# Deformable convolution plus attention on one core: five sample buffers and a second transposed chunk at the start of the first batch

## The chip, the cores and the metric

The kernel runs on one core of one Trainium2 chip, written in a tile language that schedules five engines: TensorE (PE), VectorE (DVE), ScalarE (ACT), GpSimd (POOL) and SyncE (SP, which here only issues DMAs). The metric is the device time of one execution in microseconds (us). Before the change three runs took 7757.02, 7759.71 and 7764.04 us; their median is 7759.71.

## The reference

The input is x of shape (4, 128, 64, 64) in fp32. For each batch (cut to what matters):

```
offset, mask = conv3x3(x, w_off), sigmoid(conv3x3(x, w_mask))   # after GroupNorm of x
samples      = bilinear_sample(x, grid + offset) * mask          # 9 taps, 4 corners each
x2           = x + einsum('bckhw,ock->bohw', samples, w) + bias  # deformable conv, residual
t            = layernorm(tokens of x2)                           # 4096 tokens of 128
q = k = v    = cosine / cumulative-product features of t         # 16 heads of 8
a            = softmax(q k^T / sqrt(8)) v                        # over all 4096 tokens
y            = combine, layernorm, FFN, then top-2 of 8 experts  # out has the shape of x
```

## The kernel before

**Preparing a batch.** `prepare(b)` (L784) loads x, runs `group_norm`, writes a table of corner pairs to DRAM (`corner_table`, L450 to L481), computes for each of 4096 positions and 9 taps a table row and four weights (`offsets`, in two halves of 16 blocks; L483 to L561), and then samples (`deform`, L563). The table takes 16 DMAs of 256 KB, from four row blocks `tok`; those of batch 0 go partly through ScalarE's queue, behind the loads of the weights (`load`, `load_bc`, L283 to L291, and L303 to L340), and the fourth `tok` must wait for one of three `v` buffers (L468). Ahead of `deform`, batch 0 also runs `settle` (L384): some VectorE operations on weights that the FFN needs.

**Units.** `deform` walks over 96 units: 8 chunks of 512 positions, in each 3 groups of 3 taps and 4 blocks of 128 positions. A unit, called u0, u1 and so on here, is three indirect DMAs that POOL issues (L575, 256 KB each, two units ahead, into one of three `v` buffers), a VectorE multiply by the weights (L589), and two adds (L591, L592). Then, in chunk 0 of batch 0, TensorE transposes the three taps (L600) and VectorE copies them into `sT_first` (L601). In all other chunks VectorE makes three 32x32 stream transposes (L617), SP writes the result to DRAM (`smd`, L630; four puts per group) and reads it back transposed (`sT`, L663; four loads per group).

**Chunks.** When a chunk's 12 units are done, `convolved` (L647) runs the nine-tap conv on TensorE (L273), adds the residual (`xr`, L689), normalizes (`x2`, `xt`; POOL raises to the power -0.5, L376), and `features` (L723) makes the rows `rn` on VectorE, the value rows `fx` on POOL (L754), then TensorE transposes `rn` (`fT_ps`, L767) and VectorE splits the result in `hiT` and `loT` (L769, L770). SP writes these to `kTd` and `qTd` (L777, L778), from where attention loads keys `kT` (L1156), queries `qT` (L1166) and values `qf` (L1158). All of TensorE's small work shares one PSUM bank (`misc`).

**Attention.** A step is one block of 128 keys against 512 queries for four heads: four matmuls into `sc` (L1178), two exponentials on ScalarE (L1187), four matmuls into `acc` (L1195). There are 3700 steps in all, 964 in the first batch. Batch 0's steps begin while its later chunks are still being prepared: step 0 needs chunk 0, step 16 chunk 1, step 64 chunk 2, step 104 chunk 3; this opening ends with step 160, and steps 256, 260, 288 and 292 need chunks 4 to 7.

**What sets the order.** A planner, `Beside`, steps through the attention and fits the other work between. Each piece declares its cost with `need(pe=, dve=, lat=, after=)`; `later` puts an emission off to a planned time, and `hold` keeps pieces of one PSUM bank together. The order that comes out is written for PE, DVE, SP and POOL, in the program's order (`tc.manual_schedule`); ScalarE's order is a scheduler's. Each engine runs its own list in order. DMAs share eight semaphore slots, and a DMA waits for the one eight before it.

Of the kernel before, what the change touches and what calls it, by code (L numbers as in the profile page):

```python
# [9 lines left out]
F32 = mybir.dt.float32  # L10
# [193 lines left out]
def ve(n, ops=1):  # L204

    return ops * (0.17 + n / 960.0)
# [12 lines left out]
def kernel(  # L219
# [39 lines left out]
    progress = {}  # L259
    featuring = []  # L260


    alone = []

# [15 lines left out]
    expo = cpool.tile([P, 4], F32, name="expo")  # L280
    nc.vector.memset(expo, -0.5)

    def load(ap, shape, name):  # L283
        t = cpool.tile(shape, F32, name=name)
        nc.scalar.dma_start(out=t, in_=ap)
        return t

    def load_bc(ap, n, name):
        t = cpool.tile([P, n], F32, name=name)
        nc.scalar.dma_start(out=t, in_=ap.to_broadcast([P, n]))  # L290
        return t  # L291

    gm = load(gmean, [P, P], "gm")
# [24 lines left out]
    wconv_sb = load(wconv, [P, KK, C], "wconv_sb")  # L318
    bconv_sb = load(bconv.rearrange("o c -> c o"), [P, 1], "bconv_sb")
    rx_sb = load_bc(rx, HD, "rx_sb")  # L320
    ry_sb = load_bc(ry, HD, "ry_sb")
    wcomb_sb = load(wcomb, [P, C], "wcomb_sb")
    b1_sb = load(b1, [P, FFN // P], "b1_sb")
    w2_sb = load(w2, [P, FFN // P, C], "w2_sb")
    vec_sb = cpool.tile([P, 6, C], F32, name="vec_sb")
    for i in range(6):
        nc.scalar.dma_start(out=vec_sb[:, i, :], in_=vecs[i : i + 1, :].to_broadcast([P, C]))
# [3 lines left out]
    nc.scalar.dma_start(out=rw_sb[:, :NE], in_=rw)  # L331
    rb_sb = load_bc(rb, NE, "rb_sb")
    ew_sb = load(ew, [P, NE, C], "ew_sb")
    eb_sb = load(eb, [NE, C], "eb_sb")


    w1_4 = work.tile([32, FFN], F32, tag="f2", name="w1_4", bufs=NF2)
    for i in range(4):
        nc.scalar.dma_start(out=w1_4[HD * i : HD * (i + 1), :], in_=w1)
# [86 lines left out]
    def group_norm(b, xc, got):  # L426
# [20 lines left out]
        rsqrt(rs, pv[:, 0:1], 1e-5, 1, "gn_t")  # L447
        got.extend((mg, rs))

    def corner_table(b, xc, mg, rs, tab):  # L450


        tv = tab[: TW * TW].rearrange("(y x) (k c) -> y x k c", x=TW, c=C)
        for ch in range(NBLK // 8):
            yield need(dve=ve(1024), lat=0.3)
            part = xc[:, 1024 * ch : 1024 * (ch + 1)]
            nc.vector.tensor_scalar(part, part, mg, rs, ALU.subtract, ALU.mult)
            tok = work.tile([P, 3, 4 * C], F32, tag="v", name=f"tok{b}_{ch}", bufs=NV)
            tok = tok.rearrange("p k (q c) -> p (k q) c", c=C)[:, :8]
            for i in range(0, 8, 4):  # L460
                yield need(pe=tr(4), dve=ve(512), lat=FREE)
                pt = misc(f"tok_ps{b}_{ch}_{i}")
                for n in range(4):
                    j = 8 * ch + i + n
                    nc.tensor.transpose(
                        pt[:, C * n : C * (n + 1)], xc[:, P * j : P * (j + 1)], ident
                    )
                nc.vector.tensor_copy(  # L468
                    tok[:, i : i + 4, :], pt.rearrange("p (i c) -> p i c", c=C)
                )  # L470
# [12 lines left out]
    def offsets(b, xn, idx, wt):  # L483

        xn3 = xn.rearrange("p (h w) -> p h w", w=WW)
        HB = NBLK // 2
        for half in range(2):
            blk = slice(HB * half, HB * (half + 1))

            def temp(name, n):  # L490
                return work.tile([P, HB, n], F32, tag="p2", name=f"{name}{b}_{half}", bufs=NP2)

# [23 lines left out]
            om = temp("om", 27)  # L516
            pt = misc(f"oc_ps{b}_{half}")
            for i in range(4):
                nc.tensor.transpose(
# [4 lines left out]
                pt.rearrange("p (i c k) -> p i c k", c=4, k=32)[:, :, :, :27],  # L524
            )

            yield need(dve=ve(288, 2))
            mk = temp("mk", KK)
# [5 lines left out]
            fl, up, ix = temp("fl", 18), temp("up", 18), temp("ix", KK)  # L534
# [28 lines left out]
    def deform(b, tab, idx, wt):  # L563


        AHEAD = NV - 1
# [4 lines left out]
        def gather(_, kg, j):  # L571
            v = work.tile([P, 3, 4 * C], F32, tag="v", name=f"v{b}_{j}_{kg}", bufs=NV)
            for k in range(3):
                kk = 3 * kg + k
                nc.gpsimd.indirect_dma_start(  # L575
                    out=v[:, k, :], out_offset=None, in_=tab,
                    in_offset=bass.IndirectOffsetOnAxis(ap=idx[:, j, kk : kk + 1], axis=0),
                )
            return v, beside.gathered()

        sent = 0.0
        ahead = [gather(*units[n]) for n in range(AHEAD)]
        for n, (ch, kg, j) in enumerate(units):
            progress[b] = 0.1 + 0.9 * n / len(units)
            v, landed = ahead.pop(0)
            v4 = v.rearrange("p k (q c) -> p (k q) c", c=C)
            w12 = wt[:, j, 3 * kg : 3 * kg + 3, :].rearrange("p k q -> p (k q)")
            yield need(dve=ve(1536), after=landed)
            nc.vector.tensor_tensor(v4, v4, w12[:, :, None].to_broadcast([P, 12, C]), ALU.mult)  # L589
            yield need(dve=ve(768) + ve(384))  # L590
            nc.vector.tensor_tensor(v[:, :, : 2 * C], v[:, :, : 2 * C], v[:, :, 2 * C :], ALU.add)  # L591
            nc.vector.tensor_tensor(v[:, :, :C], v[:, :, :C], v[:, :, C : 2 * C], ALU.add)  # L592
            if (b, ch) == (0, 0):

                if (kg, j) == (0, 0):
                    sT = big.tile([P, KK, CH], F32, tag="xs", name="sT_first")
                yield need(pe=tr(3), dve=ve(384))
                pt = misc(f"sT_ps{j}_{kg}")
                for k in range(3):
                    nc.tensor.transpose(pt[:, P * k : P * (k + 1)], v[:, k, :C], ident)  # L600
                nc.vector.tensor_copy(  # L601
                    sT[:, 3 * kg : 3 * kg + 3, P * j : P * (j + 1)],
                    pt[:, : 3 * P].rearrange("p (k c) -> p k c", c=P),
                )
                if n + AHEAD < len(units):
                    beside.later(beside.dve, lambda u=units[n + AHEAD]: ahead.append(gather(*u)))
                if (kg, j) == (2, 3):
                    featuring.append(True)
                    beside.add("prepare", convolved(b, ch, sT), 0.5, True)
                continue  # L610

            yield need(dve=ve(384))
# [3 lines left out]
            for k in range(3):  # L616
# [4 lines left out]
            if n + AHEAD < len(units):  # L621
                beside.later(beside.dve, lambda u=units[n + AHEAD]: ahead.append(gather(*u)))
            if j % 4 < 3:
                continue
            while kg == 0 and len(featuring) > 1:
# [25 lines left out]
    def convolved(b, ch, sT=None):  # L651
# [133 lines left out]
    def prepare(b):  # L785
# [693 lines left out]
```

## Time and profile before

| quantity | value |
|---|---|
| median of 3 runs | 7759.71 us |
| profiled execution | 7737.5 us, span 7735.7 us |
| mean granted TensorE clock | 0.964 |
| table: first and last of the final ten landings | 40.27, 52.30 us |
| fourth `tok` copied; first gather issued | 42.58; 53.47 us |
| first multiply L589 (u0); that of u11 | 69.81; 122.86 us |
| `hiT` of chunk 0; first score | 167.72; 190.07 us |
| `hiT` of chunk 1; score of step 16; of step 20 | 284.23; 304.0; 325.94 us |
| `hiT` of chunk 3; score of step 104 | 508.72; 539.02 us |
| `hiT` of chunk 7; score of step 292 | 901.19; 931.68 us |

The profiled execution lies 22.2 us below the median of the runs. The profile is of one execution; times in it count from the start of its span. "Busy" leaves out DMA issues. A bracket behind a row of a timeline names how long the engine was idle before it and what ended that.

### The profile page before, as it was taken

To read this page: it belongs to the slowest core of one execution; us is meant where nothing else is said; L and a number is where in the kernel's file an instruction comes from. 1 tells how busy PE (TensorE), PEld (TensorE's weight loads), DVE (VectorE), ACT (ScalarE), POOL (GpSimd) and SP (SyncE) were. 2 spreads that over 40 slices of the span, in tenths; PEclk is the share of its full clock that TensorE was granted. 3 is DMA by queue.
4 is the path that set the end of the run, shared out by engine and by line. 5 is a ranking of instruction groups with operands and counts; after the bars stand their busy time and mean duration, and the time that the engine had idled before them with its cause. 6 is when DMAs were issued, how large, how long until landed. Compare 5 with 4: busy or idle time off the path is not lost.

```text
span 7735.7 us, 181988 instructions
## 1 busy us (share of the span) xinstructions
PE 7156.1 (93%) x73700; PEld 2517.5 (33%) x73700; DVE 4484.8 (58%) x9000; ACT 6871.2 (89%) x7441; POOL 1648.3 (21%) x1326
## 2 busy tenths in 40 slices
PE   2579999899999999999999989989999999999997
PEld 1122232323333333333333323333333333333333
DVE  7666456666444767776554667765444545545444
ACT  0478999888999899989999988988999999999995
POOL 5454134343000432422000333431000000000000
PEclk6789999999999999999999999999999999999998
DMA  5777567978556878887766788997665587777762
GB/s 175 207 229 229 145 202 236 306 240 282 162 169 198 277 226 269 280 268 247 206 177 184 236 259 281 295 296 248 183 188 161 150 253 242 245 236 253 240 216 76
DMA packets 928758, 1735.41 MB, mean 224 GB/s; under 512 B 169458, under 2 KB 398348, under 8 KB 877228
## 3 DMA queue, kind: packets, MB, share of 16 engines
q1 hardware_dynamic: 828062, 1417.20, 60.4%
q0 software_dynamic: 92160, 302.06, 12.1%
q8 instruction: 578, 9.47, 0.5%
q10 hardware_dynamic: 7694, 4.52, 0.2%
q14 instruction: 264, 2.16, 0.1%
HBM read 1061.47 MB, written 661.93 MB: 223 GB/s over the span
## 4 chain that ended last, share of the span: by engine, by line
PE 81%; DMA 7%; DVE 4%; issue 2%; ACT 2%; SPq 2%; another core or an unknown queue 0%; POOL 0%; ACTq 0%; POOLq 0%; DVEq 0%
PE acc L1195 39%; PE sc L1178 24%; PE acc L1131 5%; PE e_ps L273 4%; PE conv_ps L273 3%; ACT e L1187 2%; PE f_ps L273 2%; DMA sT<-smd 1%; DMA et<-etd 1%; PE om_ps L507 1%; DMA etd<-st 1%; DVE v L589 1%; DMA kT<-kTd 1%; DMA qT<-qTd 1%; PE ao_ps L273 1%
## 5 line engine op out<-in xcount | busy, mean ns | idle before, releaser
L1187 ACT ACTIVATE e<-sc 128x1024 f32<-128x1024 f32 x7400 | 6868.1, 1068 | 724.7 <-PE sc L1178 470.2
L1195 PE MATMUL acc<-e,qf 128*32 128x512 f32 x29600 | 3961.1, 605 | 27.0 <-DVE cu L1399 16.2
L1178 PE MATMUL sc<-qT,kT 32*128 32x512 f32 x14800 | 2390.7, 500 | 292.4 <-ACT e L1187 153.6
L1178 PEld LDWEIGHTS sc<-qT,kT 32*128 32x128 f32 x14800 | 956.3, 183 | 3697.6 <-ACT e L1187 3078.1
L575 POOL DMA_INDIRECT v<-tab,idx x1152 | 1444.7, 1254 | 1754.5 <-DVE tr L617 1108.1
L1069 DVE STREAM_TRANSPOSE st<-e 128x1024 f32<-128x1024 f32 x792 | 937.4, 1222 | 775.5 <-ACT e L1187 606.5
L1195 PEld LDWEIGHTS acc<-e,qf 128*32 128x32 f32 x29600 | 800.4, 110 | 587.7 <-issue 329.1
L376 POOL TENSOR_TENSOR r<-ln_t,expo 128x4 f32<-128x4 f32 x96 | 112.2, 1169 | 3135.1 <-DVE ln_t L374 3096.3
L589 DVE TENSOR_TENSOR v<-v,wt 128x1536 f32<-128x1536 f32 x384 | 666.0, 1734 | 91.3 <-DMA v<-tab,idx 63.2
L1131 PE MATMUL acc<-et,qf 128*32 128x128 f32 x12672 | 521.3, 281 | 36.4 <-DMA et<-etd 30.5
L993 DVE TENSOR_TENSOR eo<-e_ps,gt 128x512 f32<-128x512 f32 x256 | 175.1, 685 | 549.6 <-PE e_ps L273 544.2
L273 PE MATMUL conv_ps<-sT,wconv_sb 128*32 128x256 f32 x4464 | 365.9, 402 | 26.4 <-DMA sT<-smd 17.9
L1131 PEld LDWEIGHTS acc<-et,qf 128*32 128x32 f32 x12672 | 302.4, 110 | 236.8 <-issue 187.1
L591 DVE TENSOR_TENSOR v<-v 128x768 f32<-128x768 f32 x384 | 367.9, 958 | 10.5
L1397 DVE COPY cu<-acc 128x512 f32<-128x512 f32 x128 | 88.5, 691 | 413.7 <-PE acc L1195 372.0
L617 DVE STREAM_TRANSPOSE tr<-v 128x128 f32<-128x128 f32 x1116 | 257.7, 282 | 40.4 <-DMA etd<-st 25.1
L592 DVE TENSOR_TENSOR v<-v 128x384 f32<-128x384 f32 x384 | 215.5, 561 | 13.3
L376 POOL TENSOR_TENSOR rstd<-lt_t,expo 128x4 f32<-128x4 f32 x32 | 57.7, 1804 | 533.2 <-DVE lt_t L374 526.2
L273 PE MATMUL f_ps<-w_sb,h 128*32 128x128 f32 x4096 | 164.8, 280 | 0.0
L878 DVE TENSOR_SCALAR h<-h_ps,b_sb 128x512 f32<-128x512 f32 x128 | 95.0, 744 | 102.5 <-PE h_ps L876 99.1
L273 PEld LDWEIGHTS conv_ps<-sT,wconv_sb 128*32 128x32 f32 x4464 | 91.4, 109 | 170.1 <-issue 151.3
L754 POOL COPY fx<-rn 128x512 f32<-128x512 f32 x32 | 28.9, 904 | 528.9 <-DVE rn L753 328.1
(224 smaller groups left out, 3041.1 us busy)
## 6 DMA issues: line engine op xcount, KB each, us to landing
etd<-st SPq DMA_DIRECT2D x1584, 256.0 KB
et<-etd SPq DMA_DIRECT2D x396, 1024.0 KB
kT<-kTd SPq DMA_DIRECT2D x400, 256.0 KB
smd<-tr SPq DMA_DIRECT2D x372, 192.0 KB
sT<-smd SPq DMA_DIRECT2D x372, 192.0 KB
qf<-fqd SPq DMA_DIRECT2D x400, 144.0 KB
qT<-qTd SPq DMA_DIRECT2D x166, 256.0 KB
atd<-cu SPq DMA_DIRECT2D x128, 256.0 KB
```

What stands on the lines that cost most here:

```text
L273: nc.tensor.matmul(dst[c : c + 32], lhsT=lhsT[:, c : c + 32], rhs=rhs, start=start, stop=stop)
L575: nc.gpsimd.indirect_dma_start(out=v[:, k, :], out_offset=None, in_=tab, in_offset=bass.IndirectOffsetOnAxis(ap=idx[:, j, kk : kk + 1], ax ...
L589: nc.vector.tensor_tensor(v4, v4, w12[:, :, None].to_broadcast([P, 12, C]), ALU.mult)
L591: nc.vector.tensor_tensor(v[:, :, : 2 * C], v[:, :, : 2 * C], v[:, :, 2 * C :], ALU.add)
L592: nc.vector.tensor_tensor(v[:, :, :C], v[:, :, :C], v[:, :, C : 2 * C], ALU.add)
L617: nc.vector.transpose(out=tr9[:, k, :, j % 4, :], in_=v[:, k, :C].rearrange("p (c i) -> p c i", i=32),)
L993: nc.vector.tensor_tensor(ws[hf], pe.rearrange("p (e c) -> p e c", c=C), gt[:, i, 4 * hf : 4 * (hf + 1), None].to_broadcast([P, 4, C]), AL ...
L1069: nc.vector.transpose(out=st[:, :, 2 * pr : 2 * pr + 2, :].rearrange("p o h (q j) -> p o (h q) j", j=32), in_=es[pr].rearrange("p h (q o i ...
L1131: nc.tensor.matmul(acc[32 * h : 32 * (h + 1), P * kt : P * (kt + 1)], lhsT=qf[:, t, QW * h : QW * h + 32], rhs=e[:, :, h, 32 * t : 32 * (t ...
L1178: nc.tensor.matmul(ps[i // 2][:, i % 2, :], lhsT=kT[h : h + 32, P * (t % 4) : P * (t % 4 + 1)], rhs=qT[h : h + 32, :], start=True, stop=True,)
L1187: nc.scalar.activation(e, ps[pr], AF.Exp, scale=1.0 / math.sqrt(HD))
L1195: nc.tensor.matmul(acc[32 * h : 32 * (h + 1), :], lhsT=qf[:, t % 4, QW * h : QW * h + 32], rhs=es[h // 2][:, h % 2, :], start=(t == ts[0]) ...
```

## The change

Only batch 0's preparation is changed.

- Thirteen groups of weights are marked late: their loads are emitted after the corner table. In the built order of ScalarE's queue twelve loads (four of `vecs`, the router's two, the experts' two, four of `w1`) stand behind the six table puts of that queue; `wconv` to the first two of `vecs` still stand ahead of them.
- `tok` of the fourth row block is a spare buffer of the tag `et`, which attention uses later.
- `offsets` is split: both halves' offset convolutions and the first half's rows and weights come first; the second half's rows and weights (`rest`, 18 VectorE operations) come after unit 11.
- The first 36 units use five buffers (three `v`, two `et`) and gather four units ahead, the others three and two as before.
- Chunk 1 also goes through TensorE's transposes, without `smd` and `sT`: 36 stream transposes, 12 puts and 12 loads go, 36 transposes and 12 copies come. A unit's copy stands behind the multiply of the next unit. Chunk 1's first transposes wait until chunk 0's conv is summed (`summed`).
- `settle` stands after unit 35 in place of before unit 0.

The core of the diff:

```diff
-        nc.scalar.dma_start(out=t, in_=ap)
+        fill(t, ap, late)
...
+    def spare(name):
+        t = work.tile([P, 4, 4, P], F32, tag="et", name=name, bufs=2)
+        return t.rearrange("p r h x -> p (r h x)")
...
+            if b == 0 and ch == 3:
+                tok = spare(f"tok{b}_{ch}").rearrange("p (i c) -> p i c", c=C)[:, :8]
...
+        yield from products(0, got)
+        yield from rows_and_weights(0, got[0])
+        yield from products(1, got)
+        rest.append(rows_and_weights(1, got[1]))
...
+        def early(n):
+            return b == 0 and n < 3 * 12
+        def gather(last):
+            nonlocal issued
+            while issued < len(units) and issued <= last + (4 if early(issued) else 2):
+                n = issued
+                issued += 1
+                _, kg, j = units[n]
+                if early(n) and n % 5 > 2:
+                    v = spare(f"v{b}_{j}_{kg}")[:, : 12 * C].rearrange("p (k q) -> p k q", k=3)
+                else:
+                    v = work.tile([P, 3, 4 * C], F32, tag="v", name=f"v{b}_{j}_{kg}", bufs=NV)
...
+            if b == 0 and n == 36:
+                yield need(dve=5.0)
+                settle()
...
             nc.vector.tensor_tensor(v4, v4, w12[:, :, None].to_broadcast([P, 12, C]), ALU.mult)
+            if moved:
+                yield need(pe=0.01, dve=ve(384))
+                moved.pop()()
...
-            if (b, ch) == (0, 0):
+            if b == 0 and ch < 2:
+                if n % 12 == 0:
+                    while len(summed) < ch:
+                        yield need(lat=0.5)
+                    sT = big.tile([P, KK, CH], F32, tag="xs", name=f"sT_first{ch}")
...
+                moved.append(move)
+                beside.later(beside.now + 0.8, lambda n=n: gather(n))
+                if n % 12 == 11:
...
+                    beside.add("prepare", convolved(b, ch, sT), 0.5, True)
+                    if ch == 0:
+                        yield from rest
...
+        summed.append(True)
...
         yield from corner_table(b, xc, *got, tab)
+        while not_yet:
+            not_yet.pop(0)()
...
-        yield from offsets(b, xc, idx, wt)
-        if b == 0:
-            settle()
-        yield from deform(b, tab, idx, wt)
+        yield from offsets(b, xc, idx, wt, rest)
+        if b > 0:
+            yield from rest[0]
+        yield from deform(b, tab, idx, wt, rest[0])
```

More of the change, by code (lines that the diff above doesn't have):

```diff
@@ L260 @@
     featuring = []
+    summed = []
     alone = []
@@ L281, with fill, emit, load @@
     nc.vector.memset(expo, -0.5)
-    def load(ap, shape, name):
+    not_yet = []
+    def fill(t, ap, late):
+        def emit():
+            nc.scalar.dma_start(out=t, in_=ap)
+        if late:
+            not_yet.append(emit)
+        else:
+            emit()
+    def load(ap, shape, name, late=False):
         t = cpool.tile(shape, F32, name=name)
-        nc.scalar.dma_start(out=t, in_=ap)
+        fill(t, ap, late)
         return t
-    def load_bc(ap, n, name):
+    def load_bc(ap, n, name, late=False):
         t = cpool.tile([P, n], F32, name=name)
-        nc.scalar.dma_start(out=t, in_=ap.to_broadcast([P, n]))
+        fill(t, ap.to_broadcast([P, n]), late)
         return t
@@ L317 @@
     grid_sb = load(grid, [P, NBLK, 18], "grid_sb")
[L318 to L324, printed above, removed]
+    wconv_sb = load(wconv, [P, KK, C], "wconv_sb", True)
+    bconv_sb = load(bconv.rearrange("o c -> c o"), [P, 1], "bconv_sb", True)
+    rx_sb = load_bc(rx, HD, "rx_sb", True)
+    ry_sb = load_bc(ry, HD, "ry_sb", True)
+    wcomb_sb = load(wcomb, [P, C], "wcomb_sb", True)
+    b1_sb = load(b1, [P, FFN // P], "b1_sb", True)
+    w2_sb = load(w2, [P, FFN // P, C], "w2_sb", True)
     vec_sb = cpool.tile([P, 6, C], F32, name="vec_sb")
     for i in range(6):
-        nc.scalar.dma_start(out=vec_sb[:, i, :], in_=vecs[i : i + 1, :].to_broadcast([P, C]))
+        fill(vec_sb[:, i, :], vecs[i : i + 1, :].to_broadcast([P, C]), True)
     b_comb, g1, beta1, b2, g2, beta2 = (vec_sb[:, i, :] for i in range(6))
@@ L330 @@
     nc.vector.memset(rw_sb, 0.0)
[L331 to L334, printed above, removed]
+    fill(rw_sb[:, :NE], rw, True)
+    rb_sb = load_bc(rb, NE, "rb_sb", True)
+    ew_sb = load(ew, [P, NE, C], "ew_sb", True)
+    eb_sb = load(eb, [NE, C], "eb_sb", True)
     w1_4 = work.tile([32, FFN], F32, tag="f2", name="w1_4", bufs=NF2)
     for i in range(4):
-        nc.scalar.dma_start(out=w1_4[HD * i : HD * (i + 1), :], in_=w1)
+        fill(w1_4[HD * i : HD * (i + 1), :], w1, True)
     is_lo = cpool.tile([32, 1], F32, name="is_lo")
@@ L457, in corner_table @@
             nc.vector.tensor_scalar(part, part, mg, rs, ALU.subtract, ALU.mult)
-            tok = work.tile([P, 3, 4 * C], F32, tag="v", name=f"tok{b}_{ch}", bufs=NV)
-            tok = tok.rearrange("p k (q c) -> p (k q) c", c=C)[:, :8]
+            if b == 0 and ch == 3:
+                tok = spare(f"tok{b}_{ch}").rearrange("p (i c) -> p i c", c=C)[:, :8]
+            else:
+                tok = work.tile([P, 3, 4 * C], F32, tag="v", name=f"tok{b}_{ch}", bufs=NV)
+                tok = tok.rearrange("p k (q c) -> p (k q) c", c=C)[:, :8]
             for i in range(0, 8, 4):
@@ L481, in corner_table, with offsets, temp, products @@
             beside.later(beside.dve, put)
-    def offsets(b, xn, idx, wt):
+    def offsets(b, xn, idx, wt, rest):
         xn3 = xn.rearrange("p (h w) -> p h w", w=WW)
         HB = NBLK // 2
[L487 to L491, printed above, removed]
+        def temp(name, n, half):
+            return work.tile([P, HB, n], F32, tag="p2", name=f"{name}{b}_{half}", bufs=NP2)
+        def products(half, got):
             for n, k in enumerate((4, 0, 1, 2, 3, 5, 6, 7, 8)):
@@ L515, in offsets @@
             yield need(pe=tr(4), dve=ve(432), lat=0.2)
-            om = temp("om", 27)
+            om = temp("om", 27, half)
+            got.append(om)
             pt = misc(f"oc_ps{b}_{half}")
@@ L525, in offsets, with rows_and_weights @@
             )
+        def rows_and_weights(half, om):
+            blk = slice(HB * half, HB * (half + 1))
             yield need(dve=ve(288, 2))
-            mk = temp("mk", KK)
+            mk = temp("mk", KK, half)
             nc.scalar.activation(mk, om[:, :, 18:27], AF.Exp, scale=-1.0)
@@ L533, in offsets @@
             yield need(dve=ve(288, 3))
-            fl, up, ix = temp("fl", 18), temp("up", 18), temp("ix", KK)
+            fl, up, ix = temp("fl", 18, half), temp("up", 18, half), temp("ix", KK, half)
             nc.vector.tensor_scalar(fl, p, ROUND, None, ALU.add)
@@ L561, in offsets, with deform @@
                     )
-    def deform(b, tab, idx, wt):
-        AHEAD = NV - 1
+        got = []
+        yield from products(0, got)
+        yield from rows_and_weights(0, got[0])
+        yield from products(1, got)
+        rest.append(rows_and_weights(1, got[1]))
+    def deform(b, tab, idx, wt, rest):
         units = [
@@ L569, in deform @@
         ]
[L571 to L579, printed above, removed]
+        ahead = []
+        issued = 0
+        def early(n):
[8 more added lines that the diff above has]
+                    v = spare(f"v{b}_{j}_{kg}")[:, : 12 * C].rearrange("p (k q) -> p k q", k=3)
+                else:
+                    v = work.tile([P, 3, 4 * C], F32, tag="v", name=f"v{b}_{j}_{kg}", bufs=NV)
+                for k in range(3):
+                    kk = 3 * kg + k
+                    nc.gpsimd.indirect_dma_start(
+                        out=v[:, k, :], out_offset=None, in_=tab,
+                        in_offset=bass.IndirectOffsetOnAxis(ap=idx[:, j, kk : kk + 1], axis=0),
+                    )
+                ahead.append((v, beside.gathered()))
         sent = 0.0
-        ahead = [gather(*units[n]) for n in range(AHEAD)]
+        moved = []
+        gather(-1)
         for n, (ch, kg, j) in enumerate(units):
             progress[b] = 0.1 + 0.9 * n / len(units)
+            if b == 0 and n == 36:
+                yield need(dve=5.0)
+                settle()
+            while not ahead:
+                yield need(lat=0.5)
             v, landed = ahead.pop(0)
@@ L592, in deform @@
             nc.vector.tensor_tensor(v[:, :, :C], v[:, :, :C], v[:, :, C : 2 * C], ALU.add)
-            if (b, ch) == (0, 0):
-                if (kg, j) == (0, 0):
-                    sT = big.tile([P, KK, CH], F32, tag="xs", name="sT_first")
-                yield need(pe=tr(3), dve=ve(384))
+            if b == 0 and ch < 2:
+                if n % 12 == 0:
+                    while len(summed) < ch:
+                        yield need(lat=0.5)
+                    sT = big.tile([P, KK, CH], F32, tag="xs", name=f"sT_first{ch}")
+                yield need(pe=tr(3), lat=FREE, hold=True)
                 pt = misc(f"sT_ps{j}_{kg}")
@@ L600, in deform, with move @@
                     nc.tensor.transpose(pt[:, P * k : P * (k + 1)], v[:, k, :C], ident)
[L601 to L607, printed above, removed]
+                def move(sT=sT, kg=kg, i=j % 4, pt=pt):
+                    nc.vector.tensor_copy(
+                        sT[:, 3 * kg : 3 * kg + 3, P * i : P * (i + 1)],
+                        pt[:, : 3 * P].rearrange("p (k c) -> p k c", c=P),
+                    )
+                moved.append(move)
+                beside.later(beside.now + 0.8, lambda n=n: gather(n))
+                if n % 12 == 11:
+                    yield need(pe=0.01, dve=ve(384))
+                    moved.pop()()
+                    while featuring:
+                        yield need(lat=0.5)
                     featuring.append(True)
                     beside.add("prepare", convolved(b, ch, sT), 0.5, True)
+                    if ch == 0:
+                        yield from rest
                 continue
@@ L620, in deform @@
                 )
-            if n + AHEAD < len(units):
-                beside.later(beside.dve, lambda u=units[n + AHEAD]: ahead.append(gather(*u)))
+            beside.later(beside.dve, lambda n=n: gather(n))
             if j % 4 < 3:
@@ L798, in prepare @@
         yield from corner_table(b, xc, *got, tab)
+        while not_yet:
+            not_yet.pop(0)()
         idx = work.tile([P, NBLK, KK], I32, tag="idx", name=f"idx{b}", bufs=1)
         wt = work.tile([P, NBLK, KK, 4], F32, tag="wt", name=f"wt{b}", bufs=1)
-        yield from offsets(b, xc, idx, wt)
-        if b == 0:
-            settle()
-        yield from deform(b, tab, idx, wt)
+        rest = []
+        yield from offsets(b, xc, idx, wt, rest)
+        if b > 0:
+            yield from rest[0]
+        yield from deform(b, tab, idx, wt, rest[0])
     def bc4(v):
```

## The prediction

> **What bounds the kernel now.** I read the page's busy shares, then the windows of the opening, then ScalarE's and TensorE's timelines and the waits there.
>
> ```profile
> PE 7156.1 (93%) x73700; PEld 2517.5 (33%) x73700; DVE 4484.8 (58%) x9000; ACT 6871.2 (89%) x7441; POOL 1648.3 (21%) x1326
> ```
>
> Over the whole span TensorE and ScalarE are nearly full, so only their idle time can be won. The windows (us; busy time and count for PE, PEld, DVE, ACT, POOL; granted clock, DMA share, GB/s) show where it lies:
>
> ```profile
> 60.00:128.00 68.00, 11.32 (x48) 6.48 (x52) 54.17 (x80) 0.00 (x0) 46.02 (x38) 0.50 0.49 146
> ...
> 190.00:304.00 114.00, 45.61 (x350) 15.43 (x350) 79.98 (x143) 30.30 (x32) 63.67 (x49) 0.65 0.74 219
> ...
> 510.00:540.00 30.00, 2.37 (x22) 0.71 (x14) 19.09 (x28) 0.38 (x2) 20.53 (x16) 0.60 1.00 298
> 540.00:920.00 380.00, 358.26 (x2844) 108.22 (x2846) 211.60 (x411) 347.03 (x375) 128.76 (x99) 0.95 0.66 196
> ```
>
> Until 304 us VectorE (54.17 of 68) and POOL prepare; from 540 on TensorE has 358.26 of 380. ScalarE's timeline (start, length, engine, line, count, [idle before, releaser]) gives the waits:
>
> ```profile
> 190.90 5.61 ACT L1187 ACTIVATE e<-sc 128x1024 f32<-128x1024 f32 x6 [132.90 <-PE sc L1178]
> ...
> 304.09 5.61 ACT L1187 ACTIVATE e<-sc 128x1024 f32<-128x1024 f32 x6 [64.10 <-PE sc L1178]
> ...
> 326.83 5.65 ACT L1187 ACTIVATE e<-sc 128x1024 f32<-128x1024 f32 x6 [14.41 <-PE sc L1178]
> ```
>
> These are step 0 (chunk 0's features), step 16 (chunk 1's) and step 20. TensorE's timeline shows the later two, steps 104 (chunk 3) and 292 (chunk 7):
>
> ```profile
> 539.02 1.22 PE L1178 MATMUL sc<-qT,kT 32*128 32x512 f32 x6 [27.63 <-DMA kT<-kTd]
> ```
> ```profile
> 931.68 0.80 PE L1178 MATMUL sc<-qT,kT 32*128 32x512 f32 x4 [9.92 <-DMA kT<-kTd]
> ```
>
> The changed order of instructions has conv and transposes of chunks 1 to 7 moved by some steps, and from step 293 on it is the old order. So the effect is what step 292 gains, carried unchanged to the end. I sum against the profiled run, 7737.5 us (span 7735.7), which is 22.2 below the median 7759.71; the gain is then taken from the median. Faster or slower counts from 0.2%, 15.5 us, about what a measurement here can tell.
>
> **1. Table and offsets: first gather 53.47 to about 51, -2.5.** VectorE's copy of the fourth row block stood behind one wait:
>
> ```profile
> DVE tok L468 <- DMA tab<-tok: 14.0, 1, 14.0
> ```
>
> The spare buffer ends it: copied near 29, not 42.58. Twelve weight loads (ScalarE's queue, 0.44 to 0.55 each in the chain, about 6 us) now stand behind the table puts; nine before them stay. But the 16 puts, landing 1.34 apart from 40.27 to 52.30, are then bounded by transfer, and the index is ready some 20 ops (7 us) after TensorE's offset conv at 40.4, which no edit speeds. Bounds -1 and -4.
>
> **2. Unit 0's multiply: 69.81 to 57.4, -12.4.** Its data was there at 59.86; VectorE was in half 1's index ops (57.67 to 64.85) and settle (64.85 to 69.8). Both go behind. Now data sets it: 51.0 + three gathers 3.75 + landing 2.6. Half 1's ops return as 7.2 us on VectorE after unit 11, beside chunk 0's conv (127.8 to 139.5 now, 11.7): cover enough; without it, +7. Settle's 5 return after unit 35, where VectorE waits on gathers; without that cover, +5.
>
> **3. Units 0 to 11: 4.82 each now, 5.0 after; 11 x 0.18 = +2, so -10.4.** Five buffers look like more room. POOL's timeline says otherwise:
>
> ```profile
> 75.65 1.55 POOL L575 DMA_INDIRECT v<-tab,idx  x1 [0.30 <-issue]
> 77.51 1.28 POOL L575 DMA_INDIRECT v<-tab,idx  x1 [0.30 <-issue]
> 79.22 0.94 POOL L575 DMA_INDIRECT v<-tab,idx  x1 [0.43 <-PE sT_ps L600]
> ...
> 132.14 2.07 POOL L575 DMA_INDIRECT v<-tab,idx  x1 [0.30 <-issue]
> 134.52 1.28 POOL L575 DMA_INDIRECT v<-tab,idx  x1 [0.30 <-issue]
> 136.10 2.06 POOL L575 DMA_INDIRECT v<-tab,idx  x1 [0.30 <-issue]
> ```
>
> Of 4.82 us POOL works or issues all but 0.13 (its wait of 0.43 less the usual 0.30). A gather is 0.95 with VectorE idle; one that starts in a two-input VectorE op (L589, 1.75; L591, 0.96; L592, 0.56) lasts until about 0.8 after it (75.65 + 1.55 = 77.20; that L589 ended at 76.39). The new buffers let POOL run on, but into more such ops: two of three gathers stalled to about 1.6 give 0.95 + 3.2 + 0.9 = 5.0. Nearest rows: 5.14 between multiplies from 169.66 to 174.85, and 1.77 per gather (5.3) from 132.14 to 146. Bounds: 3.75 (none stalled) and 7.1 (all at 2.07 + 0.30).
>
> The Trainium skill, "SBUF — State Buffer", Who interferes with whom, says that a tensor_tensor op with both inputs in SBUF contends with GpSimd's reads, and infers that descriptor generation needs the write side and so goes on. By that rule VectorE would bound a unit; the sum would be rival A. The 1.28 to 2.07 beside L589 and L591 speak against it, so I keep the row.
>
> **4. Chunk 0 to the first score: 190.07 to 179, -11.** From u11's multiply (122.86) to hiT (167.72) 44.9, to the score 22.35. L601's copy now stands behind the next unit's multiply, which hides TensorE's 0.89 of transposes (1.01 idle per unit today). Bounds -5, -16.
>
> **5. Chunk 1 through TensorE: step 16 at 304.0 to 292, -12.** Gone: 12 puts, 12 loads on SP (0.5 to 1.1 issue each), a 6.6 wait for sT, 36 stream transposes (0.23 each, 8.4). Added: 36 transposes on TensorE (12 x 0.89 = 10.7) and 12 copies of 0.56 (6.7). TensorE's are in order between scores, so a late unit holds scores behind it (u22's and u23's about 4 us), while idle 64 us per the second ScalarE wait: covered. The new wait of chunk 1's first transposes for chunk 0's conv queues them behind it on TensorE, and u12's copy and u13's adds behind it on VectorE; conv ends near 129, when u12's data is there, so it costs a unit at most, 5. On POOL unit 18's gathers now follow fx (L754; 164.3 now, 153 after), where they stood ahead of it. From there six units on POOL at 5.0 and, after the last copy of acc, VectorE's units 29 to 35 set the end; xr1 256.1 to about 237, then 30.5 to hiT and 24.5 to the score (28.1 and 19.8 today; SP has chunk 2's puts ahead of kT). Bounds -3, -20.
>
> **6. Step 20: 325.94 to 303, -23.** qT waited behind eight sT loads (14.41 idle); four stand there now. Bounds: -12 (wait stays), -26.
>
> **7. Step 104: 539.0 to 496, -43.** Chunk 3's feature transposes stand before step 98, not 104: 6 x 1.87 us (ScalarE's rate) = 11.2 earlier on top of 22.7, hiT 508.72 to 475. kT follows the puts directly, before 4 smd puts and 4 sT loads (30.3 from hiT to score now, 21 after). TensorE still waits 8 to 10 of 27.6. Rows must be ready: the features ended at 500.6 for 508.0 now; 476.8 (xr3) moves by 22.7 + 2 steps, plus 23.8 is 474, just in time. Step 71.5's loads stand behind chunk 2's puts: 0 to +4. Step 108's qT, now behind eight loads, gives -39.
>
> **8. Step 292: -39 becomes -30.** Chunk 7's feature transposes stand five steps later (282 to 287): 5 x 1.87 = +9.4 on the 9.92 wait, for its kT stays behind the same loads. What follows is unchanged. **Sum: 7737.5 - 30 = 7707.5; from the median 7759.7 - 30 = 7730.**
>
> **Forecast (0.58):** gain 20 to 40, 7720 to 7740.
>
> **Rival A (0.17): gathers are not stalled.** The unit falls to 3.96 (VectorE) or 3.75: 22 units shorter by 1.04 to 1.25, of which half to all reaches step 292: 11 to 27 more, gain 41 to 57: 7703 to 7719, centre 7711. For: 0.95 alone. Against: the stalled rows.
>
> **Rival B (0.17): chunk 3's gain is not had.** If its features are late for step 98 (no slack in 7), TensorE stands at the transposes as long as it saw idle at 104. Then -23 + 9.4 = -13; if step 20's wait stays too, -12 + 9.4 = -3. 7747 to 7757, centre 7751: no change.
>
> **Rival C (0.08), slower: gathers that always collide.** More gathers in flight beside a VectorE that no longer pauses: from T us per unit in place of 5.0, chunks 0 and 1 lose 22 x (T - 5.0). It decides from T = 5.0 + 30/22 = 6.4; at 7.1 it is +46 - 30 = +16: 7776. Against: 5.3 in the densest rows.
>
> That five buffers bring nothing by themselves is part of the forecast, not a rival: parts 1, 2, 5 and 7 don't need them.
>
> Range: C is left out, and A's and B's tails: 7700 to 7755. Faster: forecast and A, 0.75; same: B, 0.17; slower: C, 0.08.
>
> **What would show it.** First gather at 50 to 52; chunk 0's multiplies 57 to 112, 5.0 apart; first exponential near 180; no wait of 14 at step 20; TensorE's wait before step 104 of 8 to 10; before step 292 of about 19; the last score the same distance after step 292 as today. Wrong if multiplies stand 4 or 7 apart, if TensorE waits before chunk 3's transposes (B), or if a later stretch changes though its order does not.

## The result and the profile after

The changed kernel took 7728.29 us (median of 6 runs, 7714.41 to 7735.37) beside 7758.36 for the kernel before (6 runs, 7742.07 to 7764.04); ratio 0.9968, 95% interval 0.9957 to 0.9979. Two repeats, with 10 and 12 runs of the changed kernel, gave 0.9977 (0.9965 to 0.9989) and 0.9975 (0.9965 to 0.9986). By these ratios the gain is 25, 18 and 19 us. So the change makes the kernel faster, by a quarter of a per cent. The forecast of 7730 lies 2 us from the first median, but the gain that it named, 30, lies inside the interval of the first comparison alone: those of the two repeats end at 27, and their middles lie below the 20 to 40 that it called likely.

The profiled execution took 7722.5 us (span 7720.7). The profile's busy line has the same work as before, 36 matmuls more on TensorE and 24 fewer operations on VectorE:

```profile
PE 7154.7 (93%) x73736; PEld 2520.7 (33%) x73736; DVE 4480.6 (58%) x8976; ACT 6870.4 (89%) x7441; POOL 1655.8 (21%) x1326
```

The windows of the same stretches as before (us; busy time and count for PE, PEld, DVE, ACT, POOL; clock, DMA share, GB/s):

```profile
60.00:128.00 68.00, 20.90 (x159) 11.25 (x162) 50.94 (x68) 0.00 (x0) 55.32 (x42) 0.55 0.56 161
190.00:304.00 114.00, 42.60 (x362) 14.99 (x358) 87.65 (x165) 29.86 (x33) 73.46 (x53) 0.65 0.70 212
510.00:540.00 30.00, 19.96 (x180) 6.61 (x184) 11.24 (x18) 16.68 (x18) 11.18 (x8) 0.72 0.83 241
540.00:920.00 380.00, 339.17 (x2668) 102.43 (x2662) 207.06 (x405) 330.10 (x357) 120.39 (x96) 0.93 0.62 185
```

From 60 to 128 us POOL is busy 55.32 in place of 46.02: it now sets the pace, as the forecast said. From 510 to 540 TensorE works 19.96 where it worked 2.37, so chunk 3's wait has moved away. From 540 to 920 it works 19 us less than before: a wait of step 292 now falls into this window. ScalarE's timeline (start, length, [idle before, releaser]) has the waits before steps 0, 20, 104 and 108. Line numbers are those of each run's own kernel; here L1258 is the exponential, L1249 the scores, L642 the multiply and L622 the gather:

```profile
178.14 1.94 ACT L1258 ACTIVATE e<-sc 128x1024 f32<-128x1024 f32 x2 [122.49 <-PE sc L1249]
...
310.38 1.94 ACT L1258 ACTIVATE e<-sc 128x1024 f32<-128x1024 f32 x2 [4.80 <-PE sc L1249]
...
495.90 5.61 ACT L1258 ACTIVATE e<-sc 128x1024 f32<-128x1024 f32 x6 [7.00 <-PE sc L1249]
...
522.01 5.65 ACT L1258 ACTIVATE e<-sc 128x1024 f32<-128x1024 f32 x6 [17.77 <-PE sc L1249]
```

Step 0 waits 122.5 for 132.9, step 20 4.8 for 14.4. TensorE's timeline has the two places where gain is given back, step 108 (the conv of chunk 4, which stands ahead of it, and its score) and step 292 (a matmul for the next batch's norm, and its score):

```profile
514.14 1.08 PE L275 MATMUL conv_ps<-sT,wconv_sb 128*32 128x256 f32 x8 [8.45 <-DMA sT<-smd]
521.12 0.80 PE L1249 MATMUL sc<-qT,kT 32*128 32x512 f32 x4 [5.90 <-DMA qT<-qTd]
```
```profile
901.44 0.59 PE L451 MATMUL gn_pm<-gn_mv,gm 128*128 128x1 f32 x2 [9.04 <-DVE gn_mv L448]
913.12 0.80 PE L1249 MATMUL sc<-qT,kT 32*128 32x512 f32 x4 [11.09 <-DMA kT<-kTd]
```

Because every step has its exponentials on ScalarE, the start of a step's first one is a ruler through the whole execution. The forecast's times are those of the scores, about 0.9 earlier. Before2, after2, before3 and after3 are the two kernels again, the rest are the experiments below. The runs came from three chips. The columns up to x_smd1 count as the first (for before and after no chip is on record, but their pace is that of before2 and after2). The others are of two chips on which the kernel before takes 7615 us (medians of 21 and 19 runs): x_buf3, x_smd1b, x_nomul and y_two of one, before3, after3, x_both and y_best of the other. They are compared with one another only, and as no profile of before or after comes from the chip of x_buf3, those four are compared across chips.

| step | before | before2 | after | after2 | x_early | x_smd1 | faster chips: before3 | after3 | x_buf3 | x_smd1b | x_both | x_nomul | y_two | y_best |
|---|---|---|---|---|---|---|---|---|---|---|---|---|---|---|
| 0 | 190.9 | 192.5 | 178.1 | 175.6 | 178.2 | 202.7 | 188.6 | 175.9 | 173.6 | 179.3 | 180.2 | 161.6 | 172.4 | 172.8 |
| 16 | 304.1 | 303.7 | 296.4 | 296.8 | 300.3 | 312.8 | 299.8 | 288.3 | 273.0 | 296.8 | 281.5 | 274.7 | 290.2 | 289.7 |
| 20 | 326.8 | 326.1 | 310.4 | 311.3 | 320.2 | 326.0 | 323.0 | 302.6 | 284.0 | 311.6 | 292.1 | 288.4 | 304.6 | 304.6 |
| 64 | 421.4 | 422.4 | 406.9 | 413.3 | 404.8 | 422.8 | 413.5 | 398.0 | 392.7 | 408.1 | 408.1 | 382.8 | 399.6 | 402.6 |
| 104 | 539.9 | 541.0 | 495.9 | 500.5 | 518.6 | 527.9 | 529.7 | 483.9 | 515.5 | 513.6 | 526.7 | 469.7 | 484.6 | 490.7 |
| 108 | 552.0 | 552.8 | 522.0 | 524.6 | 529.7 | 544.1 | 542.1 | 505.8 | 527.0 | 525.3 | 538.6 | 493.5 | 507.6 | 499.7 |
| 288 | 913.9 | 922.5 | 883.9 | 882.1 | 906.6 | 917.4 | 890.6 | 859.9 | 890.6 | 887.2 | 901.2 | 843.6 | 854.4 | 869.0 |
| 292 | 932.6 | 942.0 | 914.0 | 912.3 | 926.5 | 936.3 | 910.2 | 890.5 | 910.1 | 906.9 | 920.5 | 873.5 | 866.7 | 884.0 |
| last | 7650.1 | 7670.1 | 7635.1 | 7630.3 | 7662.1 | 7637.5 | 7522.3 | 7505.1 | 7522.1 | 7525.5 | 7543.3 | 7488.9 | 7490.2 | 7512.9 |

After against before, by pairs of profiles:

| pair | step 0 | 16 | 20 | 104 | 108 | 288 | 292 | last |
|---|---|---|---|---|---|---|---|---|
| before, after | -12.8 | -7.7 | -16.5 | -44.0 | -30.0 | -30.1 | -18.6 | -15.0 |
| before2, after2 | -17.0 | -6.9 | -14.9 | -40.5 | -28.2 | -40.3 | -29.8 | -39.7 |
| before3, after3 | -12.7 | -11.5 | -20.4 | -45.8 | -36.3 | -30.7 | -19.7 | -17.1 |

### The profile page after: what moved, and what is told of

Same layout as the page of the kernel before. It is cut to its first block, busy times and chain, and to the rows that moved or that the text cites. A ratio compares the mean times of both kernels' runs of the same rounds, so it can differ in the third digit from the quotient of the medians.

```text
span 7720.7 us, 181988 instructions
## 1 busy us (share of the span) xinstructions
PE 7154.7 (93%) x73736; PEld 2520.7 (33%) x73736; DVE 4480.6 (58%) x8976; ACT 6870.4 (89%) x7441; POOL 1655.8 (21%) x1326
## 4 chain that ended last, share of the span: by engine, by line
PE 80%; DMA 7%; DVE 4%; issue 3%; ACT 3%; SPq 2%; another core or an unknown queue 0%; POOL 0%; ACTq 0%; POOLq 0%; DVEq 0%
PE acc L1266 39%; PE sc L1249 23%; PE acc L1202 5%; PE conv_ps L275 4%; PE e_ps L275 3%; ACT e L1258 3%; PE f_ps L275 2%; DMA et<-etd 2%; DMA sT<-smd 1%; DMA etd<-st 1%; PE om_ps L530 1%; DVE v L642 1%; DVE st L1140 0%; PE ao_ps L275 0%; DMA qT<-qTd 0%
## 5 line engine op out<-in xcount | busy, mean ns | idle before, releaser
L1258 ACT ACTIVATE e<-sc 128x1024 f32<-128x1024 f32 x7400 | 6867.2, 1068 | 712.8 <-PE sc L1249 456.0
L1249 PE MATMUL sc<-qT,kT 32*128 32x512 f32 x14800 | 2386.7, 499 | 256.0 <-ACT e L1258 158.9
L1249 PEld LDWEIGHTS sc<-qT,kT 32*128 32x128 f32 x14800 | 954.9, 183 | 3655.4 <-ACT e L1258 3087.5
L622 POOL DMA_INDIRECT v<-tab,idx x1152 | 1453.5, 1262 | 1739.0 <-DVE tr L685 1095.4
L642 DVE TENSOR_TENSOR v<-v,wt 128x1536 f32<-128x1536 f32 x384 | 665.8, 1734 | 101.3 <-DMA v<-tab,idx 78.8
L685 DVE STREAM_TRANSPOSE tr<-v 128x128 f32<-128x128 f32 x1080 | 249.4, 282 | 33.1 <-DMA etd<-st 19.9
```

Source lines behind the costliest of these rows:

```text
L622: nc.gpsimd.indirect_dma_start(out=v[:, k, :], out_offset=None, in_=tab, in_offset=bass.IndirectOffsetOnAxis(ap=idx[:, j, kk : kk + 1], ax ...
L685: nc.vector.transpose(out=tr9[:, k, :, j % 4, :], in_=v[:, k, :C].rearrange("p (c i) -> p c i", i=32),)
L1249: nc.tensor.matmul(ps[i // 2][:, i % 2, :], lhsT=kT[h : h + 32, P * (t % 4) : P * (t % 4 + 1)], rhs=qT[h : h + 32, :], start=True, stop=True,)
L1258: nc.scalar.activation(e, ps[pr], AF.Exp, scale=1.0 / math.sqrt(HD))
```

## The experiments

### The two kernels again

No edit. Three profiles of each were taken, so that what changes from run to run isn't put down to the change.

> The kernel before once more, with a second profile. Its first profile (7737.5) lies 22 us under the median of its runs. Theory: that profile was a fast one after step 292, so step 292 comes again at 932.6 within 3 us and the end is 15 to 25 us later (span 7750 to 7760). Rival: the early waits vary, and step 292 comes 8 us later or more, which would make the gain at step 292 about 28, near the forecast's 30.

> The changed kernel once more, for the size of the gain. In its first profile step 292 comes 18.6 us earlier than in the profile of before and the end 15.0 earlier, while the medians of the runs are 30 apart. Theory: the early part is steady from run to run, so step 0, 16, 104 and 292 come again within 3 us of 178.1, 296.4, 495.9 and 914.0, and the difference to the medians lies after step 292 or in before's profile. Rival: the early part itself varies by 10 us (a wait on DMAs ends now earlier, now later), and step 292 comes at 904 to 924. Ratio to before 0.996 to 0.998 under both.

> The kernel before, for a profile on the same chip as the next three. Its early part came twice within 2 us (step 0 at 190.9 and 192.5, step 104 at 539.9 and 541.0). Theory: the same here, whatever the chip's total: step 0 at 190 to 193, step 16 at 302 to 305, step 104 at 536 to 542, step 292 at 925 to 942. Rival: the chip that ran 1.7% faster in all is faster in the early part too, step 104 earlier by 10 us or more.

> The changed kernel for the size of its gain on the same chip, in five rounds. Theory (two pairs of profiles gave 18.6 to 30 at step 292, runs 18 and 30): step 104 at 496 to 500, 40 to 44 ahead of before; step 292 18 to 30 ahead; ratio to before 0.996 to 0.998. Rival: the forecast's 30 is met in full, ratio 0.9961 or less.

Before2 came at 7758.53 us, with step 104 at 541.0 for 539.9, but step 292 9.4 later and the last step 19.9 later than in the first profile: up to step 104 the two agree within 4 us, at step 110 within 1, and what comes behind varies by 9 to 20. So both theories were half right: step 292 moved, but the early waits did not. After2 gave 0.9977 and step 292 at 912.3 for 914.0, step 104 4.6 later, outside the theory's 3. On a faster chip step 104 of the kernel before came 10.3 us earlier than on the first, the rival's case, with some 6 of that won after step 16. After3 gave 0.9975 and 19.7 ahead at step 292. What follows: two pairs put the effect at step 292 at -19 and -20, the third at -30, and single profiles can't settle it, since 25 runs of the kernel before spread from 7727 to 7760. The medians of the repeats, 18 and 19 us, speak for the smaller one.

### Half 1's rows and settle back ahead of unit 0 (x_early)

```diff
-        rest.append(rows_and_weights(1, got[1]))
+        yield from rows_and_weights(1, got[1])
+        rest.append(iter(()))
...
-            if b == 0 and n == 36:
-                yield need(dve=5.0)
-                settle()
...
-        if b > 0:
-            yield from rest[0]
+        if b == 0:
+            settle()
```

> The later half's rows and weights and settle are put back ahead of unit 0, the rest of the change stays. Forecast's part 2: unit 0's multiply comes 12 us later (69 to 70 for 57.3) and step 0 about 12 later, 188 to 191; step 16 5 to 10 later than 296.4. In this kernel's order chunk 7's feature transposes stand at step 282 as before the change, not at 287, so 9 us come back at step 292: end 0 to +5 against the changed kernel. Rival: the 12 us are hidden behind gathers that start at the same time and run ahead (POOL sets the end of chunk 0), and step 0 stays within 4 us of 178.

Measured: step 0 at 178.2, so the rival holds and part 2's credit falls. VectorE's timeline shows why (of the multiplies, those of units 0 to 2 and 8):

```profile
65.28 1.76 DVE L640 TENSOR_TENSOR v<-v,wt 128x1536 f32<-128x1536 f32 x1
68.54 1.75 DVE L640 TENSOR_TENSOR v<-v,wt 128x1536 f32<-128x1536 f32 x1
72.13 1.75 DVE L640 TENSOR_TENSOR v<-v,wt 128x1536 f32<-128x1536 f32 x1
...
95.91 1.76 DVE L640 TENSOR_TENSOR v<-v,wt 128x1536 f32<-128x1536 f32 x1 [2.14 <-DMA v<-tab,idx]
```

Unit 0 is 8 us late, but three gathered units lie ready and a fourth is on its way; VectorE takes units 3.6 apart without a wait and has caught up with POOL at 95.9. The end, expected within 5 us of the changed kernel's, gives the gain back all the same: ratio 0.9996 (0.9987 to 1.0006). It goes at step 104, 518.6 for 495.9, though chunk 3's `hiT` came only 7 later (481.1 for 474.0). SP's timelines show the place. In the changed kernel chunk 3's keys are asked for directly after the puts:

```profile
485.38 1.23 SPq L846 DMA_DIRECT2D qTd<-loT  x1
492.33 0.33 SPq L1227 DMA_DIRECT2D kT<-kTd  x1
...
494.65 3.65 SPq L697 DMA_DIRECT2D smd<-tr  x4
```

In x_early twelve DMAs and the load of `xr` stand between:

```profile
488.69 1.24 SPq L844 DMA_DIRECT2D qTd<-loT  x1
490.03 5.95 SPq L695 DMA_DIRECT2D smd<-tr  x4
496.08 0.83 SPq L719 DMA_DIRECT2D xr<-in_x_dram  x1
496.96 6.89 SPq L728 DMA_DIRECT2D sT<-smd  x8
504.19 0.34 SPq L1225 DMA_DIRECT2D kT<-kTd  x1
```

From `hiT` to the exponential it takes 37.5 us there and 21.9 in the changed kernel. The 22.7 us so lost shrink to 7.7 at step 108, where x_early has no long wait, but are 21.8 again at step 160: ScalarE waits 9.7 us before step 136 (TensorE for queries) and 10.5 before step 143 (TensorE for VectorE's `cu`), where the changed kernel's first profile has no wait above 3.4. At step 292 10 us come back, as chunk 7's features stand at step 282 here.

### Three buffers (x_buf3), and both undone (x_both)

```diff
         def early(n):
-            return b == 0 and n < 3 * 12
+            return False
```

> Three buffers and two units ahead throughout, the rest of the change stays. In x_early, where unit 0's multiply came 8 us later, step 0 came at 178.2 all the same, since gathers had run ahead into five buffers and POOL set the end. Theory: buffers and the early multiply each remove the same 9.6 us of POOL's waiting, so either alone gives nearly all of it: unit 0 at 57.3, units 4.8 to 5.0 apart, step 0 at 176 to 182. Rival: the early start is worth nothing without the buffers, and step 0 comes at 187 to 192. In this kernel's order chunk 2's conv stands at steps 34 to 51 in place of 19 to 36, so step 64 should come 10 to 25 later than 407 to 413; chunk 7's features stand at 282 again.

> Three buffers and, besides, the later half's rows and settle back ahead of unit 0; x_early and x_buf3 undid these one at a time, and step 0 stayed at 178.2 and 173.6. Theory: each of the two removes the same waiting of POOL, so with both undone it is back: unit 0 at 65, units 4.8 to 5.0 apart, unit 11 at 118 to 121, step 0 at 185 to 190. Rival: what step 0 gained came from neither but from the table's earlier end and the index, and it stays at 174 to 180.

x_buf3: step 0 at 173.6, 2.3 ahead of after3 and just ahead of the theory's window; multiplies 5.0 apart from the third on. Within chunk 0 the buffers gain nothing. With both undone step 0 came at 180.2, just past the rival's window and short of the theory's 185: unit 0 at 65.0, unit 11 at 117.0. So of the 12.7 us of step 0, 8.4 stay with both undone, which leaves 4 to 7 that either of them brings alone. That is one profile, and step 0 of the unchanged pairs varies by 1.6 and 2.6 us on one chip. Neither theory had that right; what of the 8.4 is the earlier table, the earlier index or the copy's place behind the next multiply was not told apart.

Later it turns. ScalarE's timeline of x_buf3 at steps 64 and 104:

```profile
392.70 5.60 ACT L1258 ACTIVATE e<-sc 128x1024 f32<-128x1024 f32 x6 [26.76 <-PE sc L1249]
...
515.54 4.73 ACT L1258 ACTIVATE e<-sc 128x1024 f32<-128x1024 f32 x5 [35.76 <-PE sc L1249]
```

Step 20 is 19 us ahead of after3 and step 64 still 5, where it was expected 10 to 25 later; step 104 is 32 behind. In this order chunk 2's conv stands at steps 34 to 51 and chunk 3's feature transposes at 104 again. As in x_early, part of the 32 comes back at step 108 and is lost again by step 160 (30 behind). Ratio 1.0004 (0.9991 to 1.0016): in the order that is built without the buffers the change gains nothing.

### Chunk 0 without multiply and adds (x_nomul)

```diff
-            nc.vector.tensor_tensor(v4, v4, w12[...].to_broadcast([P, 12, C]), ALU.mult)
+            if b > 0 or n >= 12:
+                nc.vector.tensor_tensor(v4, v4, w12[...].to_broadcast([P, 12, C]), ALU.mult)
...
+            if b > 0 or n >= 12:
+                nc.vector.tensor_tensor(v[:, :, : 2 * C], v[:, :, : 2 * C], v[:, :, 2 * C :], ALU.add)
+                nc.vector.tensor_tensor(v[:, :, :C], v[:, :, :C], v[:, :, C : 2 * C], ALU.add)
```

> The multiply and the two adds of units 0 to 11 are left out (chunk 0's samples are then the bare first corner, unweighted); the order of everything else is the changed kernel's. Theory: gathers are stretched by VectorE's two-input ops, so without these the units come 3.75 apart (three gathers of 0.95 and 0.30 between) in place of 4.97, unit 11's copy some 13 us earlier, and step 0 at 162 to 166 for 178. Rival: POOL's pace is set by something else (DMAs, its own issue), gathers keep 1.03, 0.95 and 2.05, and step 0 stays within 3 us less the 3.3 of arithmetic of the last unit, 172 to 178.

Step 0 came at 161.6, just ahead of the theory's window. POOL's timelines of one unit, first in the changed kernel, then here:

```profile
75.12 1.02 POOL L622 DMA_INDIRECT v<-tab,idx  x1 [0.30 <-DMA v<-tab,idx]
76.45 0.94 POOL L622 DMA_INDIRECT v<-tab,idx  x1 [0.30 <-issue]
77.70 2.08 POOL L622 DMA_INDIRECT v<-tab,idx  x1 [0.31 <-issue]
```
```profile
76.72 0.95 POOL L622 DMA_INDIRECT v<-tab,idx  x1 [0.30 <-issue]
77.97 0.95 POOL L622 DMA_INDIRECT v<-tab,idx  x1 [0.30 <-DMA v<-tab,idx]
79.22 0.95 POOL L622 DMA_INDIRECT v<-tab,idx  x1 [0.30 <-issue]
```

The third gather falls from 2.08 to 0.95 and the unit from 4.97 to 3.75. So VectorE's arithmetic stretches the gathers, by 1.2 us a unit; the copies (0.56), still there, don't. The Trainium skill, "SBUF — State Buffer", Who interferes with whom, infers that descriptor generation goes on beside a tensor_tensor op with two SBUF inputs; a gather's work on POOL here does not (2.08 us for 0.95). Whether it is the reading of the indices or the writing of descriptors that waits, no run here tells.

### Chunk 1 through DRAM (x_smd1, x_smd1b)

```diff
-            if b == 0 and ch < 2:
+            if b == 0 and ch < 1:
...
+            while b == 0 and n == 12 and len(summed) < 1:
+                yield need(lat=0.5)
```

The last two lines are in x_smd1b alone.

> Chunk 1 goes through the stream transposes and DRAM again, the rest of the change stays. Forecast's part 5: without TensorE's transposes step 16 comes later, 300 to 304 for 296.4, and the wait of 14 before step 20 is back, so step 20 at 322 to 327 for 310.4. Rival: the way through TensorE gained nothing for step 16, because from step 0 to step 16 it takes 118.2 us after and took 113.2 before: then step 16 comes at 291 and step 20 at 305 to 314. Chunk 7 stands at step 282 here, 9 us less wait at step 292 under both.

> Chunk 1 through the stream transposes and DRAM, as x_smd1, but unit 12 waits for chunk 0's summed conv as it does in the changed kernel, so that six of chunk 1's units no longer stand ahead of chunk 0's residual on VectorE. Theory: that order cost x_smd1 its 24 us at step 0, and step 0 is 176 to 181 here. Then step 16 tells what TensorE's transposes are worth: by the forecast 4 to 8 (step 16 at 300 to 304, step 20 at 315 to 325); by the rival that they gain nothing before step 20, 288 to 296.

x_smd1 could not answer its question: step 0 came at 202.7, 24.5 late. VectorE had six of chunk 1's units, from 123.3 on, ahead of chunk 0's residual at 146.35 (131.31 in the changed kernel). The wait for `summed` therefore does more than keep a buffer. With it put back, x_smd1b has step 0 at 179.3, which bears that out, and step 16 at 296.8, where after3 has 175.9 and 288.3: of 8.5, 3.4 were there at step 0, which leaves some 5 for TensorE's way at step 16, and 8.9 in all at step 20. But 296.8 lies short of the 300 that the theory named, near the rival's 296, and from step 0 to step 16 after and after2 take 118.3 and 121.3 us, before and before2 113.2 and 111.2. So whether TensorE's way gains anything at step 16 is not shown. At step 104 x_smd1b is 29.8 behind, as in x_early with `kT` behind eight sT loads. Ratio 0.9996 (0.9987 to 1.0006), x_smd1 1.0001 (0.9989 to 1.0014).

### Two and three edits more (y_two, y_best)

```diff
-            nc.scalar.dma_start(out=t, in_=ap)
+            (nc.sync if late else nc.scalar).dma_start(out=t, in_=ap)
...
-        while not_yet:
-            not_yet.pop(0)()
+        beside.later(beside.dve + 0.1, weights)
...
     def prepare(b):
+        while b == 1 and any(l[0][0] == 0 and l[0][2] == NCH - 1 for l in loads[:1]):
+            yield need(lat=0.5)
...
+        if b == 0 and step == 104:
+            for r in (run + 1, run + 2):
+                if prepared.get((0, runs[r][2]), 1e9) <= beside.now:
+                    load_queries(r)
```

`weights` empties `not_yet`. The last four lines, in `at_hand`, are in y_best alone.

> The changed kernel with two edits. All late weights are loaded by SP after the table's puts, so ScalarE's exponential of the offsets (which stood behind twelve weight loads until 47.1) comes when its input is ready at 42: the index some 3.9 earlier, first gather 46 to 48 for 50.8, step 0 at 173 to 175 for 178. And the next batch's preparation waits until the keys of chunk 7 are asked for, so they stand ahead of its four x loads and five border DMAs: step 292 no longer waits 22 but 6 to 10, 12 to 16 us earlier. Theory: end 13 to 20 below the changed kernel, ratio to before 0.994 to 0.996. Rival: the keys wait on their own puts, which land last anyway, and what is gained at step 0 is lost in waits of steps 16 to 108: end within 5 of the changed kernel.

> y_two and a third edit: at step 104 the queries of the next two runs are asked for ahead of chunk 4's sT loads, so step 108 no longer waits 14 to 18 us for a queue behind eight loads. In this order chunk 7's feature transposes stand two steps later than in y_two (289 for 287). Theory: step 108 comes 8 to 12 us earlier against step 104 than in y_two (23.0 apart there; 11 to 15 here), and of that 4 go again at step 292: end 25 to 35 below the changed kernel, ratio to before 0.992 to 0.995. Rival: step 108's queries then wait for their own transfer beside the smd puts and the step gains under 4 us: ratio 0.9945 to 0.996.

y_two: ratio 0.9956 (0.9941 to 0.9971), 34 us below before, against 18 to 25 for the changed kernel; the intervals overlap. Each edit did its part. In the changed kernel ScalarE's timeline had shown the exponential directly behind the last weight loads, and the waits VectorE behind it:

```profile
43.29 3.76 ACTq L290 DMA_DIRECT2D w<-in_w_dram  x4
47.09 1.28 ACT L556 ACT_TABLE_LOAD   x1 [47.09 <-DMA tab<-tok]
48.38 0.34 ACT L556 ACTIVATE mk<-om 128x144 f32<-128x144 f32 x1
```
```profile
DVE mk L573 <- ACT mk L556: 3.9, 1, 3.9
```

In y_two it starts at 42.05, its table load done before. The first gather came at 46.99 for 50.81 (50.00 in after3), step 0 at 172.4 for 175.9. At step 292 SP and TensorE now read:

```profile
861.08 0.43 SPq L1242 DMA_DIRECT2D qT<-qTd  x1
861.62 0.42 SPq L1232 DMA_DIRECT2D kT<-kTd  x1
862.10 0.47 SPq L1234 DMA_DIRECT2D qf<-fqd  x1
862.62 2.07 SPq L859 DMA_DIRECT2D xc<-in_x_dram  x4
```
```profile
866.13 0.90 PE L1254 MATMUL sc<-qT,kT 32*128 32x512 f32 x6 [3.14 <-DMA kT<-kTd]
```

The keys go ahead of the next batch's loads, TensorE waits 3.14, and from step 288 to 292 it takes 12.3 us where after3 takes 30.6. Of the 24 us that y_two is ahead of after3 at step 292, 15 are left at the last step; its order differs in the next batch too, where the first feature transposes stand at step 455 for 452.

y_best, ratio 0.9966 (0.9954 to 0.9978), gained less than either theory had it. It took 9.0 from step 104 to 108 for 23.0 in y_two, more than was expected. But it reached step 104 6.1 later, 3.7 of that already at chunk 3's `hiT`, the rest with two query loads now ahead of the keys; and of the 8 us that it was ahead at step 108 it kept 1.7 at step 112, since step 111 now waits. From step 160 to 256 it needed 192 us where y_two needed 179. The feature transposes of chunks 4 to 6 stand four or five steps later there; whether this took the 13 us was not tested. Before and after alone spread as far on that stretch (177 to 192), and the profile of y_best is of the slowest of its eight runs, that of y_two of the fastest of its six.

## Why the prediction was right or wrong

**Parts 1 to 4, step 0: sizes right, credit wrong.** First gather 50.81 (51 forecast), unit 0 at 57.31 (57.4), units 4.98 apart (5.0), first exponential 178.1 ("near 180"). But part 1 said that the index ran on work which "no edit speeds"; in fact a wait of 3.9 for ScalarE stood in it. Part 2's 12.4 is the price of unit 0 alone, not of step 0: x_early shows that with five buffers POOL sets the end of chunk 0 though VectorE begins 8 us later. Undoing either alone costs nothing clear of the spread at step 0, undoing both 4 to 7 us; the other 8.4 of the 12.7 are not told apart. Part 4's stretch from unit 11's multiply to `hiT` did not shrink in the first pair (46.3 for 44.9); there 3.4 us were won between `hiT` and the exponential instead, which part 4 had not named.

**Part 3 and rival A: right in sum.** x_nomul shows that gathers beside VectorE's arithmetic cost 1.2 a unit more than alone, so rival A falls. But the make-up was another: of three gathers not two take 1.6, one takes 2.08 and the others 1.02 and 0.94. That this too gives 5.0 is partly luck.

**"Parts 1, 2, 5 and 7 don't need" the five buffers: wrong.** Part 7 needs the order that the planner builds with them. x_buf3, x_early and x_smd1b, each with one part undone, have step 104 32, 18 to 23 and 30 later and no gain in the end. Each changes the order of the whole, and that order has chunk 3's keys behind eight sT loads or its features six steps later. No run keeps the order and leaves out the buffers.

**Part 5: short.** Step 16 gained 7.7, 6.9 and 11.5 for 12, less than step 0 had. The conv of chunk 1 ended at 230.3, but its residual stood behind chunk 2's units on VectorE until 238.5, and from `hiT` to the score it took 26.7.

**Part 6: mis-sized.** Step 20 gained 16.5, 14.9 and 20.4 for 23; the wait fell from 14.4 to 4.8. Of the 11 that step 20 was to gain on top of step 16 it gained 8 to 9; the rest that is missing is part 5's.

**Part 7: right at step 104, mis-sized behind it.** -44.0, -40.5 and -45.8 for -43, with 7.0 of ScalarE's wait left. The failed term is "Step 108's qT, now behind eight loads, gives -39": it was -30.0, -28.2 and -36.3. The forecast added 4 us between steps 104 and 108, and 14.0, 12.3 and 9.5 were added. The eight sT loads took 8.7 us on SP; TensorE stood first at chunk 4's conv, which waits for them (8.45), and then for `qT`, which came only for the score at 521.12 (5.90). The conv's wait was not in the term.

**Part 8: right in kind, short in size.** From step 288 to 292 it took 11.5, 10.6 and 11.0 longer, for 9.4. Behind it TensorE's matmul for the next batch's norm stood ahead of the score as well (9.04). y_two shows that this price was the order's and not the features': with the keys first it is gone.

**The sum.** The forecast's -30 at step 292 was -18.6, -29.8 and -19.7. In the first pair the difference is step 108's wait (9) and 2 of chunk 7's. In the third it is 3 of step 108's, 2 of chunk 7's and 6 lost between steps 108 and 288. The second pair meets the -30 only because 12 us were gained between steps 108 and 288, which no part of the forecast named: on that stretch before2 took 7.7 longer than before, and after2 4.3 less than after. So that the time came out at 7728 for 7730 is partly luck: the six runs of before taken with it had a median of 7758, the 25 taken later on the first chip one of 7746. From step 292 to the last step, where the order is the old one, the gain changed by -4, +10 and -3 us, so "carried unchanged" holds within the spread of single profiles.

## What to carry to other kernels

Where a planner writes the order of in-order queues, a saving of a few microseconds in one stage is worth what the new order makes of it: follow SP's list to each later place where a stage begins, and price every DMA ahead of the one that is waited for. When two edits remove the same waiting, undo each alone before crediting either. And a saving at the beginning has to be followed to the last place where the order still differs.

## What the runs showed of the hardware

A gather of 0.95 us on POOL took 2.08 beside VectorE's two-input arithmetic and 0.95 again beside nothing but its copies of 0.56. Behind twelve DMA issues on ScalarE's queue an exponential came at 48.38 us, and at 42.05 when SP issued them; VectorE's wait of 3.9 for it went. Step 110 of the kernel before repeated within 1 us on one chip (that of the changed kernel within 2.6), while its last step came 20 us later in one execution than in another; and two other chips ran the kernel before 130 us or more faster at about the same mean granted clock (0.964 in the profiles of before, before2 and before3), almost all of it after step 104.
